# Hybrid convolution and attention kernel, last stage: gate intermediates in a PSUM bank, and eight rows' normalisation issued row by row

## The chip, the core and the metric

The kernel runs on one core of one Trainium2 chip. The core has five engines with a queue of instructions each: TensorE (PE, matrix products and transposes, which write to PSUM), VectorE (DVE), ScalarE (ACT), GpSimd (POOL) and SyncE (SP, which here only starts transfers). They share the on-chip memory SBUF; PSUM is a second, small memory of eight banks, each 512 float32 values long in each of 128 partitions. Each engine does its own queue in order, and waits for others by semaphores. The metric is the device time of one launch in microseconds (us), the median of several runs; smaller is better.

## What is computed

Two layers on an input of 4 images of 32 x 128 x 128. The first is a channel attention of each image with itself. The second works on its result as 16,384 tokens of 128 values, 4096 for each image as the kernel stages them: an attention without softmax, and then a mixture of eight experts of which each token uses two. Only the last part matters here:

```python
t = t + _L1_attn_ref(_ln_t(t), L1_attn_Wk, L1_attn_Wq, L1_attn_Wv)
t = t + _L1_ffn_ref(_ln_t(t), ...)

# in _L1_ffn_ref, x being the normalised tokens:
router_probs = jax.nn.softmax(x @ router_w + router_b, axis=-1)
top_p, top_i = jax.lax.top_k(router_probs, K)                 # K = 2 of E = 8
top_p = top_p / jnp.sum(top_p, axis=-1, keepdims=True)
expert_out = jnp.einsum('bnd,edc->bnec', x, expert_w) + expert_b
gathered = jnp.take_along_axis(expert_out, top_i[..., None], axis=2)
return jnp.einsum('bnk,bnkc->bnc', top_p, gathered)
```

## The kernel before

The four images are done one after the other. Most of the time goes into the first layer's attention, whose products keep TensorE busy. The second layer of an image lies beside the first layer of the next one. For the last image nothing is left to lie beside, so it has a stage of its own, `last_parts` (L1183), and that is the only place where the change has an effect on the work. It begins at about 1630 us of the span.

An image has 4096 tokens: 32 "rows" of 128 tokens, a token in each partition. `T` holds the tokens, `xn` the normalised ones. For the last image all eight experts are computed for every row and summed with gates, of which six are zero. A gate is a value per token and expert.

The steps of the last stage, with their lines:

- `attended` (L1207) puts the second layer's attention on each row (L1217 on DVE for rows 0 to 15; for rows 16 to 31 ACT copies the result out, L1219, and DVE adds it later, L1242). The parts that the router needs go into `la` (L1220).
- `close_stats` (L624, operations L630 to L640) closes the mean and variance of a group of rows: six small operations on DVE, then on POOL the power -1/2 (L164), the product `nbf` (L638) and its copy plus one, `nbo` (L640).
- `router_rows` (L806) makes the router's logits of 16 rows at a time out of `la` and the statistics, in two steps of four DVE operations (L811 to L814, L816 to L819), each on a tile of 128 x 128 (16 rows of 8 experts).
- `route` (L821) makes the gates of the 16 rows from the logits: maximum, difference, exponential on ACT (L832), then DVE finds the two largest and their weights (L834 to L853). The last one, L853, writes the gates.
- `normalise` (L642, L644) makes one row of `xn` on ACT. `transpose_tokens` (L862, L870, L866) turns four rows: PE transposes into a bank of the pool `ps_t`, which has three of them, and ACT copies the result back into `xn`.
- `product` (L1197, L1198) multiplies a row with four experts' weights into one bank; two products make a row. They go through five banks of the other pools in turn, so that a product waits for the one five before it to be read out.
- `scaled_sums` (L1135, L1141) on DVE multiplies an expert's result by its gate and adds it to the row's sum in `acc`; `scaled_rows` (L1146, L1155) on ACT multiplies the other experts' results by their gates into `tmp`; `sum_rows` (L1160, L1163 to L1167) on POOL adds two rows of these to `acc`. ACT has six experts of rows 0 to 7, five of rows 8 to 13, and four from row 14 on (`by_scalar`, L1193); DVE has the rest. Where both read one bank, DVE goes first.

In the time before row 0, the first 16 rows' logits and gates are made, and rows 0 to 15 are normalised and transposed. What is left of the second 16 rows is the generator `second_half` (L1237). It is taken one step further with each row k of the loop from row 1 on (L1286): the addition to `T` and the statistics in rows 1 to 4, `close_stats` in row 5, the first four logit operations in row 6, nothing in row 7, the other four and the exponential in row 8, the rest of `route` in rows 9, 11 and 13, and normalising (rows 9, 11, 13, 15) and transposing (rows 10, 12, 14, 16) of four rows each. All queues but POOL's follow the order in which the program issues; POOL's instructions of the statistics are held in that order too. In POOL's queue the power of the second half stands behind the sums of rows 0 to 3 and ahead of those of rows 4 and 5.

The end of the part before the loop, and the loop:

```python
            products = [product(k, h, bank(f"py_{b}_{k}_{h}")) for k in range(2) for h in range(2)]
            transpose_tokens(1)()
            normalise(range(8, 16), rsf, nbo)
            transpose_tokens(2)()
            transpose_tokens(3)()
            for k in range(KT + 4):
                if k < KT:
                    n = by_scalar(k)
                    scaled_sums(k, products[:2], 8 - n)
                    scaled_rows(k, products[:2], n)
                    products = products[2:]
```

Of the kernel before, what the change touches and what calls it, by code (L numbers as in the profile page):

```python
# [16 lines left out]
ALU = mybir.AluOpType  # L17
AX = mybir.AxisListType
# [4 lines left out]
def kernel(  # L23
# [43 lines left out]
    nc = tc.nc  # L67
# [11 lines left out]
    E = router_w.shape[1]  # L79
# [18 lines left out]
    def psum_t(name):  # L98
        return ps_t.tile([P, CH], F32, tag="pt", name=name)
# [6 lines left out]
    rank = const.tile([P, 1, E], F32, tag="rank", name="rank")  # L106
# [5 lines left out]
    rb_sb = const.tile([P, 1, E], F32, tag="rb", name="rb_sb")  # L112
# [3 lines left out]
    srw = const.tile([P, 1, E], F32, tag="srw", name="srw")  # L116
# [74 lines left out]
    def hold(name, evict, alloc=psum_t):  # L191


        while len(held) >= banks[0]:
            held[0]()
        bank = alloc(name)

        def done():
            if done in held:
                held.remove(done)  # L200
                evict(bank)

        held.append(done)
        return bank, done
# [397 lines left out]
    def layer1(b, st):  # L602
# [5 lines left out]
        rsf, nbf, nbo = (stat.tile([P, KT, 1], F32, tag=nm, name=f"{nm}_{b}", bufs=1) for nm in ("rsf", "nbf", "nbo"))  # L608
        lg = stat.tile([P, KT, E], F32, tag="lg", name=f"lg_{b}", bufs=1)
# [5 lines left out]
        gate = first  # L615
# [4 lines left out]
        def batch_stats(nm, r0, nr):  # L620
            bs = stat.tile([P, 16, 6], F32, tag="bs", name=f"bs_{nm}_{b}_{r0}")[:, :nr]
            return bs, [partial(nc.vector.bn_stats, bs[:, j, :], T[:, r0 + j, :]) for j in range(nr)]
# [19 lines left out]
        def normalise(rows, rs, nb):  # L642
            for k in rows:
                nc.scalar.activation(xn[:, k, :], T[:, k, :], AF.Identity, scale=rs[:, k, :], bias=nb[:, k, :])  # L644
# [158 lines left out]
                    bank[:, ts(j - j0, D + 2 * E)], keep[k // 4][:, ts(k % 4, P)], matx, start=True, stop=True  # L803
                )

        def router_rows(eng, r0, nr, la):  # L806

            sh = [P, nr, E]
            rows = slice(r0, r0 + nr)
            w1, w2 = (stat.tile([P, 16, E], F32, tag=nm, name=f"{nm}_{b}_{r0}", bufs=1)[:, :nr] for nm in ("lw1", "lw2"))  # L810
            eng.tensor_tensor(w1, nba[:, rows].to_broadcast(sh), srw.to_broadcast(sh), ALU.mult)  # L811
            eng.tensor_tensor(w1, la[:, :, E:], w1, ALU.subtract)
            eng.tensor_tensor(w1, w1, sda[:, rows].to_broadcast(sh), ALU.mult)
            eng.tensor_tensor(w1, w1, la[:, :, :E], ALU.add)  # L814
            yield
            eng.tensor_tensor(w2, nbf[:, rows].to_broadcast(sh), srw.to_broadcast(sh), ALU.mult)  # L816
            eng.tensor_tensor(w2, w2, rb_sb.to_broadcast(sh), ALU.add)
            eng.tensor_tensor(w1, w1, rsf[:, rows].to_broadcast(sh), ALU.mult)
            eng.tensor_tensor(lg[:, rows], w1, w2, ALU.add)  # L819

        def route(h):  # L821

            sh = [P, KT // 2, E]
            rows = slice(h * KT // 2, (h + 1) * KT // 2)
            ms, dn = (stat.tile([P, KT // 2, 1], F32, tag=nm, name=f"{nm}_{b}_{h}") for nm in ("ms", "dn"))
            pr = stat.tile(sh, F32, tag="prob", name=f"prob_{b}_{h}", bufs=1)
            mx = weight[:, 1, rows]
            o1, o2 = first[:, rows], second[:, rows]
            v = lg[:, rows]
            nc.vector.tensor_reduce(mx, v, AX.X, ALU.max)  # L830
            nc.vector.tensor_tensor(pr, v, mx.to_broadcast(sh), ALU.subtract)
            nc.scalar.activation(pr, pr, AF.Exp)  # L832
            yield
            nc.vector.scalar_tensor_tensor(o1, pr, 1.0, rank.to_broadcast(sh), ALU.is_equal, ALU.mult)  # L834
            nc.vector.tensor_reduce(ms, o1, AX.X, ALU.max)
            nc.vector.tensor_tensor(o1, o1, ms.to_broadcast(sh), ALU.is_equal)
            nc.vector.scalar_tensor_tensor(pr, o1, -2.0, pr, ALU.mult, ALU.add)
            yield
            nc.vector.tensor_reduce(mx, pr, AX.X, ALU.max)
            nc.vector.tensor_tensor(o2, pr, mx.to_broadcast(sh), ALU.is_equal)  # L840
            nc.vector.tensor_tensor(o2, o2, rank.to_broadcast(sh), ALU.mult)
            nc.vector.tensor_reduce(ms, o2, AX.X, ALU.max)
            yield
            nc.vector.tensor_tensor(o2, o2, ms.to_broadcast(sh), ALU.is_equal)
            nc.vector.tensor_scalar(dn, mx, 1.0, None, ALU.add)
            nc.vector.reciprocal(dn, dn)
            if not alone:
                nc.vector.tensor_copy(weight[:, 0, rows], dn)
                nc.vector.tensor_tensor(mx, mx, dn, ALU.mult)
                return  # L850
            nc.vector.tensor_tensor(o2, o2, mx.to_broadcast(sh), ALU.mult)
            nc.vector.tensor_tensor(o1, o1, o2, ALU.add)
            nc.vector.tensor_tensor(gate[:, rows], o1, dn.to_broadcast(sh), ALU.mult)  # L853

        def add_rows(u, j0, la, pa):
            nj = min(3, 8 - j0)
# [5 lines left out]
        def transpose_tokens(g, alloc=psum_t):  # L862

            pt, done = hold(
                f"ptf_{b}_{g}",
                lambda p: nc.scalar.activation(xn[:, ts(g, 4), :], p.rearrange("p (j t) -> p j t", t=P), AF.Copy),  # L866
                alloc,
            )
            for j in range(4):
                nc.tensor.transpose(pt[:, ts(j, P)], xn[:, 4 * g + j, :], ident)  # L870
            return done
# [297 lines left out]
        def store(g):  # L1169
            for s in range(2):  # L1170
                for r1 in range(2):
                    p0 = s * 64 + r1 * 32
                    nc.sync.dma_start(dst[s, r1, :, ts(g, 4), :], accs[g][p0 : p0 + 32])
# [9 lines left out]
        def last_parts():  # L1183
# [9 lines left out]
            def by_scalar(k):  # L1193

                return 6 if k < 8 else 5 if k < 14 else 4

            def product(k, h, bank):  # L1197
                nc.tensor.matmul(bank, xn[:, k, :], ew_sb[:, 4 * h : 4 * h + 4, :], start=True, stop=True)  # L1198
                return bank
# [4 lines left out]
            la = fpool.tile([P, KT, 2 * E], F32, tag="F", name=f"la_{b}")  # L1204
# [32 lines left out]
            def second_half():  # L1237

                bs, stats = batch_stats("f", 16, 16)
                for u in (2, 3):  # L1240
                    tg = T[:, ts(u, 8), :]
                    nc.vector.tensor_tensor(tg, tg, copies[u], ALU.add)  # L1242
                    yield
                    for j in range(8):
                        stats[8 * u - 16 + j]()
                        if j % 4 == 3:
                            yield
                close_stats("f", 16, 16, bs)
                yield
                logits = router_rows(nc.vector, 16, 16, la[:, 16:])  # L1250
                next(logits)
                yield
                yield
                for _ in logits:
                    pass
                gates = route(1)
                next(gates)
                yield
                for g in range(4, 8):
                    normalise(range(4 * g, 4 * g + 4), rsf, nbo)  # L1260
                    next(gates, None)
                    yield
                    transpose_tokens(g)()
                    yield

            rest = second_half()
            logits = router_rows(nc.vector, 0, 16, la[:, :16])
            next(logits)
            normalise(range(0, 4), rsf, nbo)
# [5 lines left out]
            gates = route(0)  # L1275
# [4 lines left out]
                pass  # L1280
            products = [product(k, h, bank(f"py_{b}_{k}_{h}")) for k in range(2) for h in range(2)]
            transpose_tokens(1)()
            normalise(range(8, 16), rsf, nbo)
            transpose_tokens(2)()
            transpose_tokens(3)()
            for k in range(KT + 4):  # L1286
                if k < KT:
                    n = by_scalar(k)
# [3 lines that stand above are left out]
                    if k + 2 < KT:  # L1292
                        products += [product(k + 2, h, bank(f"py_{b}_{k + 2}_{h}")) for h in range(2)]
                if 1 <= k <= KT and k % 2 == 0:
                    sum_rows(k // 2 - 1, by_scalar(k - 2), nc.vector if k == KT else nc.gpsimd)
                if k >= 5 and k % 4 == 1:
                    store(k // 4 - 1)
                if k >= 1:
                    next(rest, None)

# [102 lines left out]
```

## Time and profile before

| | us |
|---|---|
| median of 3 runs | 1737.0 |
| lowest and highest of them | 1736.75 and 1741.14 |
| the profiled execution | 1730.18 |
| its span in the profile | 1728.4 |

The times that the profile gives are of the one profiled execution, and are counted from the start of its span. The busy time of the engines in the last stage, from the profile's windows (start and end, length, busy time and instructions of each engine, granted clock of TensorE, share of the transfer engines, GB/s):

```profile
1646.50:1652.00 5.50, 5.44 (x10) 2.37 (x11) 5.05 (x22) 1.74 (x6) 0.00 (x0) 0.69 0.00 0
1652.00:1657.00 5.00, 3.54 (x14) 1.49 (x12) 2.53 (x10) 4.57 (x11) 0.00 (x0) 1.00 0.00 0
1657.00:1664.00 7.00, 6.66 (x16) 2.70 (x16) 5.44 (x18) 7.00 (x29) 3.54 (x4) 1.00 0.01 5
1664.00:1677.00 13.00, 10.47 (x23) 3.63 (x21) 11.66 (x28) 7.39 (x29) 12.52 (x13) 1.00 0.09 20
1677.00:1698.00 21.00, 17.86 (x47) 7.09 (x47) 18.03 (x46) 17.72 (x57) 16.03 (x19) 0.92 0.11 25
1698.00:1720.60 22.60, 22.53 (x52) 9.74 (x52) 17.72 (x52) 16.05 (x58) 18.65 (x22) 1.00 0.21 48
1720.60:1728.40 7.80, 0.00 (x0) 0.00 (x0) 2.13 (x5) 1.11 (x4) 0.64 (x1) 0.82 0.15 36
```

The columns of busy time are PE, PE's weight loads, DVE, ACT and POOL. A row of tokens is two products, and each product appears as two records of PE. In the first window PE does the products of rows 0 and 1; in the second ACT is the engine that works most; in the fourth DVE and POOL are busy for nearly all of the time and ACT for little more than half; in the sixth PE has no gap.

### The profile page before, as it was taken

The numbers are of one execution on the slowest core, as the hardware profiler recorded it, in microseconds if no ns is written. First come the engines' busy times: TensorE is split into PE (matmuls) and PEld (weight loads), VectorE is DVE, ScalarE is ACT, GpSimd is POOL, SyncE is SP. The second block draws the span as 40 slices with busy tenths as digits, with TensorE's granted clock in tenths as the row PEclk, the third lists the DMA queues.
The fourth block names the chain that finished last, engine by engine and source line by source line (L and its number), as shares of the span: only waits on it lengthen the run. The fifth ranks groups of instructions, "written<-read, shape, count | busy, mean of one in ns | idle before, by whom it ended". The sixth has DMA issues, their size and how long they took to land. (4 is left out here: it accounts for less than half of the span.)

```text
span 1728.4 us, 21211 instructions
## 1 busy us (share of the span) xinstructions
PE 1656.8 (96%) x5458; PEld 876.9 (51%) x5458; DVE 939.3 (54%) x2443; ACT 925.8 (54%) x2893; POOL 511.8 (30%) x553
## 2 busy tenths in 40 slices
PE   7999999999999999989999999999999999999887
PEld 4444444455554456445564455545555445544633
DVE  4433334367485235467568334557748524455686
ACT  3555445465565455446565544546656545545376
POOL 1000000011026514550014631652102650453156
PEclk9999999999999999989999999999999999999999
DMA  4775778876569899996568979998656988995001
GB/s 128 202 206 170 205 208 238 250 213 183 158 195 271 241 259 262 246 257 182 168 189 228 277 230 262 283 252 231 183 163 196 269 242 260 269 259 135 1 13 38
DMA packets 240681, 355.25 MB, mean 206 GB/s; under 512 B 27312, under 2 KB 155312, under 8 KB 226480
## 3 DMA queue, kind: packets, MB, share of 16 engines
q1 hardware_dynamic: 220048, 314.91, 64.5%
q0 software_dynamic: 12288, 25.19, 4.9%
q10 hardware_dynamic: 8224, 13.77, 2.8%
q8 instruction: 46, 0.75, 0.2%
q14 instruction: 75, 0.61, 0.1%
HBM read 183.64 MB, written 173.15 MB: 206 GB/s over the span
## 5 line engine op out<-in xcount | busy, mean ns | idle before, releaser
L559 ACT ACTIVATE pr<-pe 128x512 f32<-128x512 f32 (+1 forms) x576 | 322.4, 560 | 557.0 <-PE pe L556 428.8
L440 PE MATMUL po<-pr,qT 128*128 128x512 f32 (+3 forms) x1152 | 552.9, 562 | 3.9 <-ACT o L445 3.4
L375 PE MATMUL pg<-G,qT 128*128 128x512 f32 x880 | 453.4, 597 | 14.1 <-DMA G<-blocks 8.7
L556 PE MATMUL pe<-qn,qn 128*128 128x512 f32 x896 | 462.5, 598 | 3.3 <-ACT pr L559 3.0
L369 DVE STREAM_TRANSPOSE F<-pr 128x512 f32<-128x512 f32 x440 | 306.1, 702 | 156.1 <-ACT pr L559 132.1
L440 PEld LDWEIGHTS po<-pr,qT 128*128 128x128 f32 x1152 | 216.6, 191 | 251.8 <-issue 224.4
L380 ACT ACTIVATE junk<-G 128x512 bf16<-128x512 f32 x440 | 273.0, 621 | 7.1 <-DMA G<-blocks 7.0
L375 PEld LDWEIGHTS pg<-G,qT 128*128 128x128 f32 x880 | 167.5, 192 | 214.0 <-issue 187.0
L1114 POOL DMA_INDIRECT yb<-ys,place x192 | 185.5, 966 | 262.5 <-DMA xn<-xs 96.3
L989 POOL DMA_INDIRECT xs<-xn,place x192 | 186.1, 969 | 132.2 <-ACT pr L559 55.3
L556 PEld LDWEIGHTS pe<-qn,qn 128*128 128x128 f32 x896 | 155.3, 192 | 115.9 <-issue 103.0
L385 DVE TENSOR_TENSOR o<-o,pg 128x512 f32<-128x512 f32 x110 | 75.5, 686 | 203.1 <-PE pg L375 164.6
L164 POOL TENSOR_TENSOR rn<-ss,neg_half 128x8 f32<-128x8 f32 (+1 forms) x17 | 26.9, 1586 | 334.1 <-DVE ss L325 334.1
L559 ACT ACTIVATION_READ_ACCUMULATOR pr<-pe 128x1 f32 x576 | 112.1, 195 | 0.0
L1023 ACT ACTIVATE xn<-pys 128x256 f32<-128x256 f32 (+1 forms) x120 | 45.0, 377 | 118.3 <-PE pys L1056 67.7
L1049 PEld LDWEIGHTS pys<-ew_sb,xn 128*128 128x128 f32 x468 | 68.5, 192 | 56.3 <-issue 39.0
L164 POOL TENSOR_TENSOR rsf<-dm_f,neg_half 128x8 f32<-128x8 f32 (+1 forms) x15 | 26.2, 1748 | 233.7 <-DVE sv_f L636 233.7
L556 PE MATMUL pe<-qn 128*128 128x512 f32 (+3 forms) x256 | 91.1, 438 | 0.7 <-ACT qn L344 0.7
L164 POOL TENSOR_TENSOR rsa<-dm_a,neg_half 128x8 f32<-128x8 f32 x16 | 26.4, 1650 | 219.3 <-DVE sv_a L636 219.0
L380 ACT ACTIVATION_READ_ACCUMULATOR junk<-G 128x1 f32 x440 | 84.4, 192 | 0.0
L1049 PE MATMUL pys<-ew_sb,xn 128*128 x468 | 72.1, 277 | 11.1 <-ACT xn L1023 11.0
L1032 DVE COPY result<-pys 128x256 f32<-128x256 f32 (+1 forms) x60 | 24.6, 411 | 96.5 <-ACT xn L1023 48.7
(189 smaller groups left out, 1607.6 us busy)
## 6 DMA issues: line engine op xcount, KB each, us to landing
blocks<-F SPq DMA_DIRECT2D x108, 1024.0 KB
G<-blocks SPq DMA_DIRECT2D x432, 256.0 KB
xn<-xs SPq DMA_DIRECT2D x114, 128.0 KB
below<-F SPq DMA_DIRECT2D x31, 384.0 KB
G<-below SPq DMA_DIRECT2D x124, 96.0 KB
out_dram<-acc SPq DMA_DIRECT2D x128, 64.0 KB
xx<-in_x_dram SPq DMA_DIRECT2D x62, 128.0 KB
ys<-xn SPq DMA_DIRECT2D x60, 128.0 KB
```

Of the source, the lines that this page charges most:

```text
L164: pinned(nc.gpsimd.tensor_tensor(dst, src, neg_half.to_broadcast(list(src.shape)), ALU.pow))
L369: f()
L375: nc.tensor.matmul(pg.rearrange("p (a f) -> p a f", a=4), st["qT"][i][:, ib, :], G[:, :, ib], start=(ib == 0), stop=(ib == NJ - 1),)
L380: nc.scalar.activation(junk, G[:, :, ib], AF.Copy, accum_out=st["sums"][:, NJ * i + ib, jc : jc + 1])
L385: nc.vector.tensor_tensor(o, o, pg.rearrange("p (a j c) -> p a j c", a=4, c=S), ALU.add)
L440: nc.tensor.matmul(row["po"][:, lo:hi], qT[blk // NJ][:, blk % NJ, :], w, start=start, stop=(row["left"] == 0))
L556: nc.tensor.matmul(pe[:, c0:], qn[jc][:, ts(j, P)], qn[i][:, c0:], start=True, stop=True)
L559: nc.scalar.activation(pr[:, c0:], pe[:, c0:], AF.Exp, accum_out=sums[:, t, i : i + 1]).ins
L989: inst = nc.gpsimd.indirect_dma_start(xs[h], offset(place[:, i, k : k + 1]), xn[:, k, :], None)
L1023: nc.scalar.activation(bufs[4 + g % 2][:, :n], p[:, : n * P].rearrange("p (j t) -> p j t", t=P), AF.Copy)
L1049: nc.tensor.matmul(p[:, 2 * P + j * D : 2 * P + j * D + D], bufs[4 + g % 2][:, j, :], weights[:, bass.ds(begins[2 * (g % 2) + j], D)], sta ...
L1114: inst = nc.gpsimd.indirect_dma_start(yb[k // 4][:, i, k % 4, :], None, ys, offset(place[:, i, k : k + 1]))
```

## The change

It has two parts. First, `router_rows` and `route` take an optional tile for intermediate values. For the second 16 rows it is a bank of PSUM from the pool `ps_t` (the one that the transposes of tokens use), cut into four parts of 128 x 128. The logits, the probabilities, the ranks and the second choice of these rows are kept there instead of in SBUF. Of the values that were tiles before, `lw2` (the bias with the mean's share), the first choice `o1`, the maxima and the gates stay in SBUF. The operations and their number stay as they are. For the first 16 rows the tiles are as before, except that the sum of both choices is written over the second choice and no longer over the first. Second, the normalising of rows 8 to 15 and the transposing of its two groups are taken out of the part before the loop; row k of the loop, for k from 0 to 7, normalises row 8 + k on ACT after its own scaled rows, and after rows 3 and 7 a group of four is transposed and copied back.

```diff
-        def router_rows(eng, r0, nr, la):
+        def router_rows(eng, r0, nr, la, temps=None):
...
             w1, w2 = (stat.tile([P, 16, E], F32, tag=nm, name=f"{nm}_{b}_{r0}", bufs=1)[:, :nr] for nm in ("lw1", "lw2"))
+            w0, sums = w2, lg[:, rows]
+            if temps is not None:
+                w1, w0, sums = temps[:, 0], temps[:, 1], temps[:, 0]
...
-            eng.tensor_tensor(w2, nbf[:, rows].to_broadcast(sh), srw.to_broadcast(sh), ALU.mult)
-            eng.tensor_tensor(w2, w2, rb_sb.to_broadcast(sh), ALU.add)
+            eng.tensor_tensor(w0, nbf[:, rows].to_broadcast(sh), srw.to_broadcast(sh), ALU.mult)
+            eng.tensor_tensor(w2, w0, rb_sb.to_broadcast(sh), ALU.add)
             eng.tensor_tensor(w1, w1, rsf[:, rows].to_broadcast(sh), ALU.mult)
-            eng.tensor_tensor(lg[:, rows], w1, w2, ALU.add)
+            eng.tensor_tensor(sums, w1, w2, ALU.add)
 
-        def route(h):
+        def route(h, temps=None):
...
             v = lg[:, rows]
+            ranks = o1
+            if temps is not None:
+                v, ranks, pr, o2 = (temps[:, n] for n in range(4))
...
-            nc.vector.scalar_tensor_tensor(o1, pr, 1.0, rank.to_broadcast(sh), ALU.is_equal, ALU.mult)
-            nc.vector.tensor_reduce(ms, o1, AX.X, ALU.max)
-            nc.vector.tensor_tensor(o1, o1, ms.to_broadcast(sh), ALU.is_equal)
+            nc.vector.scalar_tensor_tensor(ranks, pr, 1.0, rank.to_broadcast(sh), ALU.is_equal, ALU.mult)
+            nc.vector.tensor_reduce(ms, ranks, AX.X, ALU.max)
+            nc.vector.tensor_tensor(o1, ranks, ms.to_broadcast(sh), ALU.is_equal)
...
-            nc.vector.tensor_tensor(o1, o1, o2, ALU.add)
-            nc.vector.tensor_tensor(gate[:, rows], o1, dn.to_broadcast(sh), ALU.mult)
+            nc.vector.tensor_tensor(o2, o1, o2, ALU.add)
+            nc.vector.tensor_tensor(gate[:, rows], o2, dn.to_broadcast(sh), ALU.mult)
...
-                logits = router_rows(nc.vector, 16, 16, la[:, 16:])
+
+                temps = psum_t("gates").rearrange("p (n k e) -> p n k e", n=4, e=E)
+                logits = router_rows(nc.vector, 16, 16, la[:, 16:], temps)
...
-                gates = route(1)
+                gates = route(1, temps)
...
             transpose_tokens(1)()
-            normalise(range(8, 16), rsf, nbo)
-            transpose_tokens(2)()
-            transpose_tokens(3)()
             for k in range(KT + 4):
...
                 if k >= 5 and k % 4 == 1:
                     store(k // 4 - 1)
+                if k < 8:
+                    normalise(range(8 + k, 9 + k), rsf, nbo)
+                    if k % 4 == 3:
+                        transpose_tokens(2 + k // 4)()
                 if k >= 1:
                     next(rest, None)
```

## The prediction

> **What bounds the kernel now.** First the page's head and its engine line, to see how long the profiled execution was and which engine is nearest to full; then the chain of waits from its end; then the timeline of VectorE (DVE) and GpSimd (POOL) where that chain leaves TensorE (PE).
>
> ```profile
> span 1728.4 us, 21211 instructions
> PE 1656.8 (96%) x5458; PEld 876.9 (51%) x5458; DVE 939.3 (54%) x2443; ACT 925.8 (54%) x2893; POOL 511.8 (30%) x553
> ```
>
> PE is busy for 96% of the span, but the edit touches only the last 75 us, so its value has to be read there. The end of the chain (start, length, engine, tile, line, instructions):
>
> ```profile
> 1646.56 5.40 PE py L1198 x8
> 1653.03 3.07 ACT xn L644 x8
> 1656.10 1.02 ACT xn L866 x2
> 1657.69 5.61 PE py L1198 x12
> 1664.59 1.69 DVE dm_f L633
> 1668.60 2.94 POOL rsf L164
> 1672.48 1.83 DVE lw L818
> 1676.87 1.55 DVE first L834
> 1690.42 2.81 PE py L1198 x6
> 1694.30 1.04 ACT tmp L1155 x4
> 1695.34 1.52 ACT xn L644 x4
> 1696.86 1.04 ACT tmp L1155 x4
> 1697.94 22.60 PE py L1198 x52
> ```
>
> From 1697.94 PE runs without a gap: 52 records are 26 products, two for each of rows 19 to 31, 22.60/26 = 0.87 us each. Whatever puts row 19's product earlier moves the end by as much. Before that the path lies on ScalarE (ACT) at 1653 and 1656, then on DVE and POOL from 1664 to about 1690, which is where the two parts of the change lie. Why DVE is slow there is in the timeline (start, length, engine, line):
>
> ```profile
> 1646.48 0.28 DVE L818 TENSOR_TENSOR lw<-lw,rsf 128x128 f32<-128x128 f32 x1
> ...
> 1672.25 1.90 POOL L1163 TENSOR_TENSOR tmp<-tmp 128x768 f32<-128x768 f32 x1
> 1672.40 1.90 DVE L818 TENSOR_TENSOR lw<-lw,rsf 128x128 f32<-128x128 f32 x1
> ...
> 1675.87 0.31 ACT L832 ACTIVATE prob<-prob 128x128 f32<-128x128 f32 x1 [2.77 <-DVE prob L831]
> ...
> 1676.44 1.81 POOL L1163 TENSOR_TENSOR tmp<-tmp 128x768 f32<-128x768 f32 x1
> 1676.78 1.62 DVE L834 SCALAR_TENSOR_TENSOR first<-prob,rank 128x128 f32<-128x128 f32 x1
> ```
>
> The same operation takes 0.28 us for the first half of the rows, with POOL idle, and 1.90 us for the second, where it ends 0.15 us after POOL's addition (1674.30 against 1674.15). L834 likewise (0.27 in the first half, 1.62 here). The bracket on the exponential shows the cost: ACT stands for 2.77 us until DVE brings the logits, and behind the exponential row 9 is queued. Row 9's first ACT instruction starts at 1676.96, though row 8's ended at 1673.09.
>
> [...] L1141 (PSUM, T and a per-row factor) stays at 0.34 to 0.35 us all through POOL's additions. [...] Here ACT's part of a row waits for DVE's on the same bank (the waits between 1652 and 1698 list ACT L1155 after DVE L1141 for 4.1 us in 4 cases).
>
> **Part one, normalising of rows 8 to 15 spread.** Before, after row 7's transposed copy, ACT runs eight normalises (3.17 us from 1652.93) and two evictions of transposes to 1657.02, and only then row 0; PE has its eight transposes before row 2's products (1656.32). After, row 0 starts when DVE has done its two operations on the same bank: 1652.96 + 0.35, about 1653.4. ACT's work to the end of row 8, from its own pitches: 36 scalings in 9.41 us are 0.261 each; normalises 3.08/8 = 0.385; an eviction 0.50 (1652.43 to 1652.93). Rows 0 to 7 have 8x6 scalings = 12.5, eight normalises 3.1, two evictions 1.0, and row 8 five scalings 1.3: 17.9. Before each eviction ACT has to wait for the transposes, of which the last needs the normalise just issued: the later groups of this kind show 0.68 us of idle time; two of 0.65 are taken, 1.3. Row 8 ends at 1653.4 + 19.2 = 1672.6, against 1673.09: by itself this part brings ACT only 0.5 us. No SP or POOL instruction is passed in program order, and POOL's list is the same; only its start moves.
>
> It brings DVE more. Row 2's product no longer stands behind eight transposes, so DVE's gap of 2.65 us before row 2 (1657.38) closes to about nothing: row 2 at 1654.8. Then the addition to T at 1655.5, before POOL starts (rows 0 and 1 leave ACT at about 1656.9), row 5 at 1659.8 and close_stats at 1660.5 instead of 1663.97. I leave close_stats at its measured 3.1 us with the waits on POOL in it (0.9 for the first half without them), since POOL is as busy: ready at 1663.6. POOL's two sums of rows 0 to 3, 4.07 us each, end at 1665.2, then L164 at 2.97 and nbf 0.3: 1668.5, where DVE needs it. DVE meanwhile does row 6, the first four logit operations (1.4 plus 0.7 for L811, which keeps two SBUF inputs), rows 7 and 8: to 1668.0.
>
> **Part two, intermediate values in PSUM.** Count and form stay: eight logit operations, then reductions, comparisons, products. For 18 of them the second tensor input is now PSUM or there is none; L811 and L816 still read two SBUF tensors. What they lose are POOL waits, their measured length minus the first half's 0.29: L818 1.62, L834 1.34, L852 0.48, L819 0.48, L812, L837 and L841 0.41 each, L851 0.37, L844 0.31, L836 0.16, L840 0.12, L831 0.08: 6.2 us of DVE. [...] The trace has no DVE write to PSUM; below 0.29 us there is no reason to go, above I allow 0.16 more each (0.45), and take a pitch of 0.38 as for L1141. From 1668.5, L816 and five more need 0.3 + 5x0.38 = 2.2: the logits are ready at 1670.7, before ACT has done row 8 at 1672.6. So the exponential no longer waits for DVE but for its turn: 1672.7, and row 9 at 1673.0 instead of 1676.96: 4.0 us gained.
>
> The bank itself comes from the three that take turns for transposes; two remain, and a transpose is evicted before the next is issued, so I cost its loss at nothing. Were a bank waited for, it would be one eviction and some hand-over, about 0.7 us for each of five transposes.
>
> **Rows 9 to 16.** Before: 1676.96 to 1698.34 on ACT, 21.4 us. ACT's own work: rows 9 to 13 25 scalings, rows 14 to 16 12, 37x0.261 = 9.7; sixteen normalises 6.2; four evictions 2.0: 17.9. The other 3.5 are 1.21 behind DVE at row 10 and four waits on transposes (0.68, 0.68, 0.71 and none). DVE after the exponential: L834 to L837 4x0.38, then row 10 done by about 1675.7, while ACT gets to row 10 at 1673.0 + 1.3 + 1.5 = 1675.8: the 1.21 goes. Two transposes still keep their 0.65; the third was late because DVE and PE were behind in row 14, so about half. That is 17.9 + 1.7 = 19.6, ending at 1692.6: 5.7 us earlier than 1698.34. PE then has the same 26 products (22.6) and the same 7.9 us of last sums and stores.
>
> Sum: 0.5 from ACT's earlier start, 3.5 from the exponential, 1.7 from rows 10 to 16 = 5.7. The profiled execution took 1730.18 us (1.8 beside its span) and would take 1724.5. The runs' median is 1737.0, 6.8 above that execution; the saving is in the last stage and is taken off unchanged: **1731.3**.
>
> **Rivals.**
> - DVE remains the bound. For: L811, L816 and all of close_stats still meet POOL, now busy from 1656.9 instead of 1660.30, and slack at the exponential is 1.9 us. If DVE meets two more of POOL's 1.8 us additions and pays 0.45 per moved operation, logits come at 1670.7 + 3.6 + 0.5 = 1674.8, row 9 at 1675.2 (1.8 gained), and rows 10 to 16 bring 1.2: 3.0, 1734.0. Against: each wait needs POOL to be just starting.
> - PSUM operands don't free DVE. Then L818 and L834 keep 1.6 and 1.3, logits at about 1672.7 (still in time for row 8), but row 10 waits about 1.8 behind L834 to L837 and the third transpose stays late: 3.7, 1733.3. This is the change not doing what it says. Against: L1141.
> - More: transposes are ready in time throughout and row 14's wait goes wholly, 1.8 more, 1729.5.
> - Slower, by PE's clock. Between 1646.5 and 1652 the windows show a granted clock of 0.69, and four products took 5.40 us, 1.35 each. If ACT's slower pace in rows 0 to 7 (1.96 us a row against PE's 1.73) makes PE's gaps so regular that this clock lasts through row 18, 34 products take 45.9 and six groups of transposes 5: from 1652.4 to 1703.4 against 1697.9, so 5.5 later: 1742.5. It decides below a clock of about 33.0/45.5 = 0.73 (29.4 us of products and 3.6 of transposes in 45.5). Against: the windows have 0.92 from 1677 to 1698 with PE busy for 85%.
>
> **How the numbers follow.** ACT as the bound 0.60; DVE 0.20; PSUM without effect 0.09; more 0.05; slower 0.06. A change under 0.3% (5.2 us) can't be told from none, so 1731.8 divides: my forecast lies close by it, about 0.62 of its chance below; with the larger gain and a little of the rivals, faster 0.45, same 0.48, slower 0.07. The forecast's own range is 1729.5 to 1733.5; the rivals on the small side and the unknown PSUM write widen it to 1728.0 to 1736.5.
>
> **What would show it.** Right: operations on the new bank at 0.30 to 0.45 us beside POOL's additions; ACT's exponential directly behind row 8, with no idle time on DVE's account; row 0 on ACT near 1653.4; the unbroken run of 52 product records starting near 1692. Wrong: the exponential still waiting for DVE; long operations with PSUM inputs; a clock under 0.8 from 1653 to 1692; or ACT waiting over 0.7 us for a transpose.

## The result, and the profile after

The changed kernel takes 1728.26 us (median of 9 runs, 1717.52 to 1735.09) against 1735.19 us (9 runs, 1729.58 to 1741.14) for the kernel before. The ratio on record is 0.9945, with a 95% interval of 0.9919 to 0.9972, so the kernel is faster, by about half a per cent; the two medians by themselves give 0.9960. Their difference is 6.9 us; the forecast was a saving of 5.7. The interval holds savings from 4.9 to 14.1 us, so its nearer end lies close to the 5.2 us that were set as the limit of what can be told from no change.

The page of the profiled execution, head and engine line:

```profile
span 1715.7 us, 21208 instructions
PE 1652.0 (96%) x5458; PEld 873.5 (51%) x5458; DVE 933.5 (54%) x2443; ACT 926.0 (54%) x2893; POOL 511.7 (30%) x553
```

This span is 12.7 us shorter than before's 1728.4, but not all of it is the change. The last stage's first expert product starts at 1646.56 before and at 1640.74 after: 5.8 us lie ahead of the stage, where both kernels do the same work. In the experiments below that same start falls anywhere from 1630.1 to 1652.3, and three executions of the changed kernel have it at 1640.74, 1648.38 and 1631.85. From the first product to the end of the span, on the other hand, these three take 74.96, 74.92 and 74.95 us. Much of the difference ahead goes with the chip: the experiments ran on three, and the start lies between 1630.1 and 1639.5 on one, 1631.9 and 1636.1 on another, 1648.3 and 1652.3 on the third. So everything below is measured in that stage, from its first expert product: **81.84 us before, 74.96 after, 6.88 saved.**

The chain of waits of after, for the same part as was shown of before (start, length, engine, tile, line, instructions; from L806 on, after's line numbers are 6 higher, so L1198 became L1204 and L1155 became L1161):

```profile
1648.20 6.93 PE py L1204 x14
...
1656.94 6.92 PE py L1204 x14
...
1665.01 1.40 ACT tmp L1161 x5
1666.58 1.31 ACT tmp L1161 x5
1667.89 1.09 ACT xn L644 x3
1669.72 1.12 PE py L1204 x2
...
1681.26 3.70 PE py L1204 x8
1685.40 22.60 PE py L1204 x52
```

The steps on DVE and POOL between 1664 and 1690 (`dm_f`, `rsf`, `lw`, `first`) are gone. From row 8 on the path goes back and forth between ACT's scalings and normalises and PE's products, and the unbroken 52 records start 44.66 us after the first product instead of 51.38. From there to the end it is 30.46 us before and 30.30 after: nothing to speak of has changed.

The timeline of after, where POOL's addition for rows 4 and 5 meets the second gates (start, length, engine, line, what is written from what):

```profile
1663.05 1.81 POOL L1169 TENSOR_TENSOR tmp<-tmp 128x768 f32<-128x768 f32 x1
...
1663.33 0.30 DVE L821 TENSOR_TENSOR gates<-gates,rsf 128x128 f32<-128x128 f32 x1
...
1664.32 0.30 DVE L837 TENSOR_TENSOR gates<-gates,weight 128x128 f32<-128x128 f32 x1
...
1666.27 0.31 ACT L838 ACTIVATE gates<-gates 128x128 f32<-128x128 f32 x1
...
1666.46 0.91 ACT L1161 ACTIVATE tmp<-py,first 128x128 f32<-128x128 f32 x3
1666.61 0.30 DVE L840 SCALAR_TENSOR_TENSOR gates<-gates,rank 128x128 f32<-128x128 f32 x1 [0.97 <-ACT gates L838]
```

L821, the old L818, took 1.90 us beside the same addition; it now takes 0.30 and ends before POOL does. The logits, less their maximum, are ready at 1664.62, 1.65 us before ACT comes to the exponential at 1666.27. The bracket has changed sides: ACT used to wait 2.77 us for DVE, and now DVE waits 0.97 us for ACT. Row 9 on ACT starts at 1666.46, hard behind the exponential.

What is left of ACT's waits on the transposes is in ACT's timeline of after (the bracket is the idle time before, and what ended it):

```profile
1655.78 0.60 ACT L872 ACTIVATE xn<-ptf 128x512 f32<-128x512 f32 x1 [0.42 <-PE ptf L876]
...
1664.52 0.60 ACT L872 ACTIVATE xn<-ptf 128x512 f32<-128x512 f32 x1 [0.42 <-PE ptf L876]
...
1671.38 0.60 ACT L872 ACTIVATE xn<-ptf 128x512 f32<-128x512 f32 x1 [0.68 <-PE ptf L876]
...
1676.76 0.60 ACT L872 ACTIVATE xn<-ptf 128x512 f32<-128x512 f32 x1 [0.68 <-PE ptf L876]
...
1681.17 0.60 ACT L872 ACTIVATE xn<-ptf 128x512 f32<-128x512 f32 x1
```

Four waits, 2.2 us together; the copy at 1681.17 waits for nothing, where its counterpart before waited 0.71.

### The profile page after: what moved, and what is told of

Its sections match the earlier page's. It is cut to its first block, busy times and chain, and to the rows that moved or that the text cites. A ratio compares the mean times of both kernels' runs of the same rounds, so it can differ in the third digit from the quotient of the medians.

```text
span 1715.7 us, 21208 instructions
## 1 busy us (share of the span) xinstructions
PE 1652.0 (96%) x5458; PEld 873.5 (51%) x5458; DVE 933.5 (54%) x2443; ACT 926.0 (54%) x2893; POOL 511.7 (30%) x553
```

## The experiments

Nine kernels are made from the changed one, and it was itself profiled twice more. The diffs below are against the changed kernel. The measure is the stage, from its first expert product to the end of the span. "Exponential" is the start of the second half's exponential on ACT, and "row 9" that of row 9's first scaling on ACT, both counted from the first product. Each line is one profiled execution, of before too; only after has three, and their stages agree within 0.04 us. All times are in us.

| kernel | span | first product | stage | exponential | row 9 |
|---|---|---|---|---|---|
| before | 1728.4 | 1646.56 | 81.84 | 29.31 | 30.40 |
| after | 1715.7 | 1640.74 | 74.96 | 25.53 | 25.72 |
| spreading alone | 1709.8 | 1630.10 | 79.70 | 25.92 | 26.96 |
| bank alone | 1710.8 | 1633.01 | 77.79 | 27.19 | 28.28 |
| copies one row later | 1712.2 | 1639.51 | 72.69 | 24.24 | 24.94 |
| the same, and rows 16 to 31 one by one | 1706.7 | 1634.09 | 72.61 | 24.92 | 25.11 |
| DVE plus 4 reductions | 1726.4 | 1651.29 | 75.11 | 25.52 | 25.74 |
| DVE plus 12 reductions | 1724.9 | 1648.34 | 76.56 | 26.28 | 27.30 |
| probe of operands | 1735.2 | 1652.31 | 82.89 | 25.46 | 25.65 |
| after, again | 1723.3 | 1648.38 | 74.92 | 25.47 | 25.67 |
| rows one by one, and another `tmp` buffer | 1707.3 | 1636.10 | 71.20 | 24.26 | 24.95 |
| the same, and gate steps one row later | 1705.7 | 1634.69 | 71.01 | 24.04 | 24.95 |
| after, timed again | 1706.8 | 1631.85 | 74.95 | 25.51 | 25.71 |

### Spreading alone

```diff
-                temps = psum_t("gates").rearrange("p (n k e) -> p n k e", n=4, e=E)
-                logits = router_rows(nc.vector, 16, 16, la[:, 16:], temps)
+                logits = router_rows(nc.vector, 16, 16, la[:, 16:])
...
-                gates = route(1, temps)
+                gates = route(1)
```

> The changed kernel with the intermediate values of the second gates back in SBUF; only the spreading of rows 8 to 15 is left. Measure: the last stage, from the first product of experts to the end of the span, 81.8 us before and 75.0 after, since the rest of the program varies by more from run to run. Theory A [...]: VectorE's operations with two SBUF inputs again end with GpSimd's additions (1.6 to 1.9 us for the third logit operation and for the first rank operation), row 10 on ScalarE waits for VectorE again, and the stage is about 78.1, 3.7 less than before. Theory B (place of the values is of no account, an earlier start is all): 75.0.

Measured: a stage of 79.70 us, and 0.9978 of the time before (0.9966 to 0.9990). The timeline of this kernel:

```profile
1652.39 1.91 POOL L1169 TENSOR_TENSOR tmp<-tmp 128x768 f32<-128x768 f32 x1
1652.55 1.90 DVE L821 TENSOR_TENSOR lw<-lw,rsf 128x128 f32<-128x128 f32 x1
...
1661.24 1.40 ACT L1161 ACTIVATE tmp<-py,first 128x128 f32<-128x128 f32 x5 [1.27 <-DVE acc L1147]
1661.66 1.98 PE L1204 MATMUL py<-ew_sb,xn 128*128 128x512 f32 x2 [2.03 <-ACT tmp L1161]
...
1663.43 1.06 PE L876 MATMUL ptf<-ident,xn 128*128 128x128 f32 x4
...
1664.59 0.60 ACT L872 ACTIVATE xn<-ptf 128x512 f32<-128x512 f32 x1 [1.96 <-PE ptf L876]
```

With the operands back in SBUF, L821 takes 1.90 us again and ends 0.15 us after POOL's addition, and row 10's scalings wait 1.27 us for DVE. So the bank is what takes this contention away, and spreading by itself saves only 2.1 us. The stage is 1.6 us longer than the 78.1 expected, and the last three lines say where most of that is: after idling for 2.03 us PE needs 1.98 us for two records that take 1.12 in after (1669.72 in its chain), and 1.06 for four transposes that take 0.60 there. ACT then stands for 1.96 us at a copy that waits 0.68 in after, 1.3 more, which is what the two groups lost. The windows view of this kernel (from : to, length, then busy us and count of PE, PE's weight loads, DVE, ACT and POOL, then the granted TensorE clock, the DMA share and GB/s) shows the reason:

```profile
1661.60:1663.60 2.00, 1.94 (x3) 0.81 (x4) 1.86 (x6) 1.04 (x5) 1.92 (x4) 0.55 0.56 130
```

The clock granted to PE was 0.55 there. So a wait of PE behind ACT and DVE (2.03 us here) can be followed by a lower clock that costs more (1.3 us here), for which the prediction's sum had no term. That it need not be is seen at the end of this document, at a wait of 2.46 us.

### The bank alone

```diff
+            normalise(range(8, 16), rsf, nbo)
+            transpose_tokens(2)()
+            transpose_tokens(3)()
             for k in range(KT + 4):
...
-                if k < 8:
-                    normalise(range(8 + k, 9 + k), rsf, nbo)
-                    if k % 4 == 3:
-                        transpose_tokens(2 + k // 4)()
```

> The changed kernel with rows 8 to 15 normalised and transposed ahead of row 0 again; only the intermediate values in PSUM are left. Theory A: VectorE's logit and gate operations take 0.3 us each beside GpSimd; the statistics are ready as late as before, the logits about 2 us after them, so the exponential follows row 8 by under 1 us instead of 2.8; with the wait at row 10 gone the stage is about 77.6. Theory B: 81.8 as before.

Measured: 77.79 us, 0.9964 of the time before (0.9949 to 0.9979). The timeline:

```profile
1658.60 1.80 POOL L1169 TENSOR_TENSOR tmp<-tmp 128x768 f32<-128x768 f32 x1
...
1658.88 0.30 DVE L821 TENSOR_TENSOR gates<-gates,rsf 128x128 f32<-128x128 f32 x1
...
1660.20 0.26 ACT L838 ACTIVATE gates<-gates 128x128 f32<-128x128 f32 x1 [0.41 <-DVE gates L837]
```

L821 is at 0.30 beside POOL without the spreading, and the exponential's wait falls from 2.77 to 0.41. The bank saves 4.05 us, spreading 2.1, both together 6.88. Both are causes, and the table says where each one works. Up to row 9 on ACT spreading gains 3.4 us, the bank 2.1 and both 4.7. From there to the end the bank gains 1.9 and both 2.2, while spreading alone loses 1.3, as much as its slow stretch of PE cost; apart from that it changes nothing there. The same 1.3 us account for it that both together save 0.7 more than the sum of the two: without them spreading would have saved 3.4 and the sum would be 7.5. (Where several executions were timed, here and below, the stage's saving as a share of the time lies inside the interval of the measured ratio.) That the operands' place does nothing is refuted by this kernel and by spreading alone.

### Which operand's place counts

In rows 21 to 28 this kernel adds three DVE operations a row beside POOL's sums, which differ only in where the operands lie. `probe` is a PSUM bank; `second` and `lg` are SBUF tiles that nothing reads any more.

```diff
+                if 21 <= k < 29:
+                    nc.vector.tensor_tensor(in_psum, flat, in_sbuf, ALU.add)
+                    nc.vector.tensor_tensor(out_psum, in_psum, in_sbuf, ALU.add)
+                    nc.vector.tensor_tensor(flat, flat, in_sbuf, ALU.max)
```

> The changed kernel with three more VectorE operations of 128x128 in each of rows 21 to 28, beside GpSimd's additions, results unused by the output except that the first rows' second choices are overwritten after their last use: two SBUF inputs into PSUM, one PSUM and one SBUF input into PSUM, two SBUF inputs into SBUF. Theory A: the number of SBUF inputs decides: the first and third wait for the running addition (means of 0.6 to 0.9 us, the longest 1.2 or more), the second stays at 0.30. Theory D: the place that is written decides: the first also stays at 0.30.

The groups of instructions by line of this kernel (line, engine, operation, out and in, count | busy us, mean ns of one | idle us before):

```profile
L1314 DVE TENSOR_TENSOR probe<-second,lg 128x128 f32<-128x128 f32 x8 | 5.4, 670 | 0.0
L1316 DVE TENSOR_TENSOR second<-second,lg 128x128 f32<-128x128 f32 x8 | 4.9, 616 | 0.0
L1315 DVE TENSOR_TENSOR probe<-probe,lg 128x128 f32<-128x128 f32 x8 | 2.4, 299 | 0.3
```

With two SBUF inputs the operation takes 0.67 us written to PSUM and 0.62 written to SBUF (the eight of the first lie between 0.29 and 1.11, of the second between 0.55 and 1.04); with one of the inputs in PSUM it takes 0.30, and the eight lie between 299 and 300 ns. So for this operation it is the input that counts, not the place of the result. The three stood in the same order in every row, but the operations that were moved in after show the same 0.30 elsewhere. The 24 added operations made the stage 7.9 us longer, so its length says nothing here.

### Slack of DVE ahead of the exponential

Two kernels add reductions of the bank on DVE between the logits and the maximum, 4 in the one and 12 in the other:

```diff
+                extra = stat.tile([P, 4, 16], F32, tag="extra", name="extra")
+                for i in range(4):
+                    nc.vector.tensor_reduce(extra[:, i % 4], temps[:, 0], AX.X, ALU.max)
                 gates = route(1, temps)
```

> The changed kernel with four more reductions of the logits on VectorE (PSUM input, 0.33 us each, 1.3 together, result unused) just ahead of the gates' first operation. Theory A (ScalarE reaches the exponential last, VectorE has slack): the exponential doesn't move; row 9's part of VectorE comes 0.5 us too late for ScalarE: stage 75.0 plus 0.5. Theory C (VectorE is still what bounds): all 1.3 us appear, 76.3.

> The same with twelve reductions, 4.0 us. Theory A: slack of 1.65 us at the exponential and 0.8 at row 9 is used up first, so the exponential comes 2.3 us later and row 9 3.2 later: stage about 78.2. Theory C: 79.0.

Measured: 75.11 and 76.56 us, 0.15 and 1.6 above after. The reductions were cheaper than assumed. The timeline of the kernel with 12:

```profile
1671.58 2.47 DVE L1266 TENSOR_REDUCE extra<-gates 128x16 f32<-128x128 f32 x12
...
1674.62 0.26 ACT L838 ACTIVATE gates<-gates 128x128 f32<-128x128 f32 x1 [0.66 <-DVE gates L837]
...
1675.64 1.40 ACT L1161 ACTIVATE tmp<-py,first 128x128 f32<-128x128 f32 x5 [0.76 <-DVE acc L1147]
```

Twelve take 2.47 us, and the four 0.89: about 0.2 each, where the 0.33 assumed was the pitch of operations of which each needs the one before (in after L837, which reads L836's maxima, starts 0.33 after it). So 0.8 and 2.4 us were added, and 0.15 and 1.6 came out. With 4 the exponential stays where it was; with 12 it moves by 0.75, which is 2.4 less the 1.65 of slack read off the profile of after, and row 9 by 1.6, which is 2.4 less the 0.8 expected there; the stage follows row 9. Were DVE the bound, 0.8 and 2.4 would have come out. DVE has its slack.

### Copies back to `xn` one row later

If ACT is the bound, its four waits on transposes are worth their full length. Here the copy of four turned rows is issued after the next row's scalings:

```diff
+            turned = []
...
                     scaled_rows(k, products[:2], n)
+                    while turned:
+                        turned.pop()()
...
-                        transpose_tokens(2 + k // 4)()
+                        turned.append(transpose_tokens(2 + k // 4))
```

(In `second_half` likewise.)

> The changed kernel, with ScalarE's copies of the transposes of groups 2 to 7 issued one row later, so that it never waits for TensorE. If ScalarE is what bounds rows 0 to 16 after the change, its waits before the copies (twice 0.42 and twice 0.68, 2.2 us) come off: stage 72.8. If VectorE or TensorE is, at most 0.5 us come off: 74.5 or more.

Measured: 72.69 us; 0.9937 of the time before (0.9917 to 0.9958). 72.8 was expected if ACT is the bound. The four waits were 2.2 us, and 2.27 came off: in after ACT is the bound up to row 16.

### Rows 16 to 31 normalised one by one

On top of the last, `second_half` normalises one row a step instead of four rows every other step, and takes a step of `route` at every second row.

```diff
-                for g in range(4, 8):
-                    normalise(range(4 * g, 4 * g + 4), rsf, nbo)
-                    next(gates, None)
-                    yield
-                    transpose_tokens(g)()
+                for r in range(16, 32):
+                    normalise(range(r, r + 1), rsf, nbo)
+                    if r % 2 == 0:
+                        next(gates, None)
+                    if r % 4 == 3:
+                        turned.append(transpose_tokens(r // 4))
                     yield
```

> As the kernel with later copies, and rows 16 to 31 also normalised one per row of the loop, rows 9 to 24, instead of four at a time in rows 9, 11, 13 and 15. If ScalarE bounds, its load for a row falls to 1.69 us in rows 9 to 13 and 1.43 from row 14, under TensorE's 1.73 and a share of a transpose, and TensorE takes over from row 9: about 10 rows at 1.88 instead of 19.5 us for eight, less a wait of about 1.3 for GpSimd near row 18: stage 72 to 71.5, about 3 to 3.5 less than the changed kernel. If VectorE bounds, no gain over the later copies alone.

Measured: 72.61 us; 0.9950 of the time before (0.9933 to 0.9968). It brought nothing beyond the last, where about 1 us was expected if ACT is the bound; the number is the one expected if DVE is. ACT's timeline of this kernel:

```profile
1653.51 1.66 ACT L1161 ACTIVATE tmp<-py,first 128x128 f32<-128x128 f32 x6 [0.48 <-DVE acc L1147]
...
1661.87 1.40 ACT L1161 ACTIVATE tmp<-py,first 128x128 f32<-128x128 f32 x5 [0.77 <-DVE acc L1147]
...
1677.57 1.14 ACT L1161 ACTIVATE tmp<-py,first 128x128 f32<-128x128 f32 x4 [1.79 <-POOL acc L1173]
```

New waits stand in place of the old: for DVE in rows 6 and 10, and in row 18 for a buffer of `tmp` that POOL still has to add up. Which of these is to blame the next kernel decides.

### Another buffer for `tmp`, and the gate steps one row later

The first of these takes row pairs with four ACT experts from the buffers of those with more, which are free by then; the second adds a shift of `route`'s steps by one row (its diff is against the first).

```diff
-                if n <= 4:
-                    tmps[k // 2] = work.tile([P, 2, n, D], F32, tag="wide", name=nm)
-                else:
-                    tmps[k // 2] = gpool.tile([P, 2, n, D], F32, tag="G", name=nm)
+                tmps[k // 2] = gpool.tile([P, 2, n, D], F32, tag="G", name=nm)
```

```diff
-                    if r % 2 == 0:
+                    if r % 2 == 1:
                         next(gates, None)
```

> The kernel that normalises row by row, with ScalarE's scaled rows from row 14 on in the pool of three buffers that rows 0 to 13 use, and not in that of two. If its small gain (stage 72.6 against 72.7 of the later copies alone) is because row 18 waits 1.79 us for GpSimd to give a buffer back, that wait goes and the stage is 71.0 to 71.5. If VectorE, which has no gap from row 3 to row 13 there, is the bound, the stage stays within 0.3 of 72.6.

> The same, with the three later steps of the second gates behind VectorE's part of rows 10, 12 and 14 instead of ahead of it. VectorE has something to do while ScalarE makes the exponential, and row 10 on ScalarE no longer waits 0.77 us for it: 0.3 to 0.8 us less than with three buffers. If TensorE bounds by then: no difference.

Measured: 71.20 and 71.01 us; 0.9941 (0.9923 to 0.9958) and 0.9938 (0.9923 to 0.9953) of the time before. The first is as expected: POOL's wait was worth 1.4 of its 1.79, so it was this wait, and not DVE, that kept the kernel before it at 72.6. The second brought 0.2 where 0.3 to 0.8 or nothing was expected: row 10's wait for DVE, 0.51 in the first, is gone, and one of 0.48 for POOL has come at 1665.23. The windows view of the first says why little is left:

```profile
1659.10:1682.90 23.80, 23.67 (x61) 10.37 (x62) 20.69 (x66) 22.50 (x78) 22.94 (x27) 1.00 0.14 33
```

From the products of row 10 on, PE is busy for 23.67 of 23.80 us at a granted clock of 1.00: here TensorE has become the bound, as it was of rows 19 to 31 all along.

### The changed kernel again

> The changed kernel as it is, for a second profile of it: if the 12.7 us between the two profiled spans are 6.9 of the last stage and 5.8 of chance in what lies ahead, the stage is 75.0 within 0.3 again and the time ahead of it falls anywhere between 1638 and 1650.

> The changed kernel once more, timed beside the kernel before and the two others on the same chip: the last stage 74.9 again, and a ratio of 0.996, 6.9 us of some 1720 to 1735, if nothing but the last stage differs; 0.9945 if what lies ahead of it also became shorter.

Measured: 74.92 and 74.95 us for the stage, and 1648.38 for the time ahead of it in the first, all as expected. The second, timed beside the two kernels of the last section, gave 0.9953 (0.9938 to 0.9969), with medians of 1709.31 and 1717.89 us. The stage's saving is 6.88/1717.9, a ratio of 0.9960, which lies inside that interval; both ratios expected, 0.996 and 0.9945, do too, so this run doesn't tell whether the 6.9 us are all of the saving or there is a little more ahead of the stage. The last kernel's stage is 3.9 us shorter than after's, but its interval (0.9923 to 0.9953) overlaps after's: that it beats the changed kernel in time is seen in the stage and not in the timing.

## Why the prediction was right in its mechanism and short in its size

- **What bounds the stage.** Right. The exponential held up by DVE, and row 9 behind it, was the largest single loss. Either part takes most of the exponential's wait away (2.77 before, 0.30 with spreading alone, 0.41 with the bank alone), but row 9 on ACT then still waits for DVE, 0.73 and 0.82 against 0.78 before; with both parts there is neither wait.
- **Part one: "by itself this part brings ACT only 0.5 us. It brings DVE more."** Right in kind: spreading alone brought row 9 forward by 3.4 us and saved 2.1. Row 0 on ACT came 6.78 us after the first product; 6.84 was forecast. The two waits on transposes were put too high: "two of 0.65 are taken, 1.3". They are 0.42 each, 0.46 less together. They were sized by the later groups, whose transposes stand in PE's queue behind a product that waits for a free bank (in after the product starts at 1669.72 and the transposes at 1670.69); here PE has turned three rows of the group by the time the fourth is normalised, and only that one is left to wait for.
- **Part two.** Right: the operations on the bank take 0.30 us beside POOL. That one input in PSUM would be enough was the author's estimate; of the profile of before only L1141, at 0.34 to 0.35 us throughout, spoke for it, and the probe shows it (0.30 us with one SBUF input, 0.67 with two). A pitch of 0.38 was forecast, and L840's next starts 0.34 after it. That excess cost nothing, since DVE had its slack. The path through DVE and POOL is met closely: counted from the first product, DVE was to have POOL's `nbf` at 21.9 us and the logits at 24.1, and had them at 21.93 and 23.88. Two SBUF inputs are still waited for where they are left: in the statistics L632 takes 1.83 us beside POOL's addition of 1.80 at 1655.26, and `close_stats` took 3.8 us (1654.91 to 1658.70) where 3.1 were allowed, but POOL was at its sums until 1659.36 and couldn't have begun on it sooner. The bank taken from the transposes' three cost nothing either: with the copies moved, the four waits came off with the same two banks, so none of them was for a bank.
- **"1672.7, and row 9 at 1673.0".** Counted from the first product that is 26.1 and 26.44; measured were 25.53 and 25.72. Of this 0.7 us, 0.46 are the two waits above; the other 0.26 lies mostly in the step from row 8 to row 9, for which 0.4 was allowed: the exponential starts at 1666.27, while row 8's last scaling is still ending (1666.42), and row 9 follows 0.19 us after the exponential's start.
- **Rows 9 to 16.** 19.6 forecast, 19.47 measured (1666.46 to 1685.93): the wait for DVE at row 10 gone and the third wait on transposes gone wholly, both as said or a little better.
- **Where it failed.** The likeliest outcome of the forecast was that no difference could be told (0.48, against 0.45 for faster), and the kernel is faster. The step that failed is the size of terms in the sum of ACT's path, above all "two of 0.65 are taken, 1.3", which measured 0.84, and the step to row 9, 0.26 too long. The forecast of 5.7 us stood only 0.5 above the 5.2 that divide the two outcomes, and these two terms alone are 0.7. With 0.1 in rows 9 to 16, and 0.3 between row 16 on ACT and the end of the span, they make up the difference between 5.7 and 6.88. All erred to the same side, so they added up instead of cancelling. With chances as even as these, and a limit so near, which of the two outcomes was put first was also a matter of luck.
- **The rivals.** "DVE remains the bound" falls by the added reductions: 0.8 us on DVE gave 0.15. "PSUM operands don't free DVE" falls by the probe, 299 ns against 670, and by spreading alone, which is that rival made into a kernel: it saved 2.1, not 3.7, and 1.3 of the difference came from PE's slow stretch. "More" was nearest in size (7.5): row 14's wait did go, though the other four stayed. "Slower, by PE's clock" falls by the windows of before and of after, and by one more line of before:

```profile
1652.00:1676.90 24.90, 20.66 (x50) 7.83 (x48) 19.53 (x54) 18.92 (x65) 15.96 (x16) 1.00 0.05 12
1676.90:1697.94 21.04, 17.80 (x46) 7.04 (x46) 18.07 (x46) 17.70 (x57) 16.07 (x19) 0.92 0.11 25
1677.30:1680.80 3.50, 3.41 (x4) 0.92 (x4) 3.33 (x7) 2.58 (x9) 3.34 (x5) 0.57 0.00 0
...
1681.52 1.12 PE L1198 MATMUL py<-ew_sb,xn 128*128 128x512 f32 x2 [0.73 <-ACT tmp L1155]
```

```profile
1646.20:1666.40 20.20, 19.01 (x48) 6.36 (x46) 17.42 (x53) 18.64 (x65) 14.59 (x14) 1.00 0.06 15
1666.40:1685.40 19.00, 17.51 (x49) 7.19 (x48) 14.45 (x46) 17.60 (x58) 17.02 (x20) 1.00 0.12 28
1685.40:1708.00 22.60, 22.58 (x52) 9.72 (x52) 17.86 (x52) 16.17 (x57) 18.64 (x22) 1.00 0.20 48
```

Before (the first fence), the 0.92 of its second row comes from the 3.5 us of the third: PE had stood still for 2.68 us behind the exponential, and then two products took 3.41 us at a clock of 0.57, where two take 1.7 at a clock of 1.00 (0.87 each from 1697.94 on). This cost the stage nothing that the trace shows: afterwards PE stood still for another 0.73 us, until ACT had read a bank (the last line). After (the second fence), no gap of PE in the loop is over 0.8 us and the clock is 1.00 throughout.

Spreading alone is the only kernel here whose stage is seen to become longer through the clock (0.55, 1.3 us). It was profiled once; that its other executions lose the same 1.3 us isn't shown.

## What to carry to other kernels

Where DVE runs beside GpSimd, look for DVE operations with two SBUF tensor inputs that end together with a GpSimd instruction (in before L818 took 1.90 us and ended 0.15 after POOL's addition), and put one of the inputs in PSUM, if a bank can be spared (0.30 us then); the result's place was indifferent here (0.67 us into PSUM and 0.62 into SBUF, both inputs being in SBUF). Then ask which engine is late next and what its own small waits are: here it was ACT, and moving four copies by one row brought another 2.3 us, where DVE had 1.65 us to spare. And compare stages, counted from an event inside them, when the time ahead of them varies by more than the effect.

## What was not expected of the hardware

- PSUM operands cost DVE nothing to speak of here. In after's two halves most 128x128 operations take 0.28 to 0.29 us on SBUF, and 0.28 to 0.30 with a PSUM input, a PSUM result, or both; the largest differences are L840 (0.27 and 0.30) and L857 (0.23 and 0.27). The 0.35 of the gated addition L1141, from which the prediction took its pitch of 0.38, is therefore not due to PSUM: L840 also reads PSUM and takes 0.30. Its per-row factor may be the difference, which wasn't tried.
- DVE operations that don't depend on each other followed at 0.2 us (12 reductions in 2.47 us; in before L818 starts 0.21 after L817), dependent ones at 0.32 to 0.33 (in before L817 starts 0.32 after L816, whose result it reads).
- PE's granted clock fell to half behind gaps of 2.68 and of 0.69 us, and the gap's length alone doesn't decide it. In short windows it is 0.50 for 3.4 us in before (1677.8 to 1681.2), soon after a gap of 2.68 us; in spreading alone, soon after one of 2.03, it is 0.55 from 1661.6 to 1663.6 and 0.83 from 1664.2 to 1667.2. In after it is 0.51 for 3.4 us (1641.3 to 1644.7) within the first four products, behind a gap of 0.69. In the run "after, timed again" those products, behind the same gap, took 3.70 us instead of 5.40, and a gap of 2.46 us came next:

```profile
1639.31 6.92 PE L1204 MATMUL py<-ew_sb,xn 128*128 128x512 f32 x14 [2.46 <-ACT tmp L1161]
```

These 14 records took 6.92 us, as they did in the first profile of after behind a gap of 0.77 (6.93, the first line of its chain). The stages of the two are 74.95 and 74.96, so the slow start didn't lengthen the stage. A gap of 2.03 us was followed by the lower clock (0.55), and behind one of 2.46 the records took as long as at the clock of 1.00 that after had from 1646.2 to 1666.4. What decides it these runs don't show.
